# One product for values and router logits behind each norm, values kept in memory, the first sequence used in place, and down products with the last tile last

## The chip, the cores and the metric

The kernel runs on one core of a Trainium2 chip. The metric is device time in microseconds, as the median of several runs. TensorE (PE, with its weight loads as PEld), VectorE (DVE), ScalarE (ACT), GpSimd (POOL) and the DMA queue's engine SyncE (SP) each work through their own list of instructions in order and wait for each other through semaphores.

## What is computed

One transformer block over 16 sequences of 512 tokens of width 256, in float32: a layer norm, local attention with 16 heads of 16 (a token sees itself and the 128 tokens ahead of it), a mixture of 8 experts with 2 chosen for each token, a shared expert for all tokens, and the residual.

```python
xn = _layernorm(x)
# attention
q = (xn @ Wq.T + bq).reshape(B, S, 16, 16); k, v likewise
scores = where(local_mask, q k^T / 4, -10000.0)
attn = softmax(scores) + 1e-9
a = (attn v).reshape(B, S, 256) @ Wo.T + bo
# experts
logits = xn @ gate_w.T
_, idx = top_k(logits + beta, 2)
probs = sigmoid(logits at idx)
eo = (silu(xn gate_proj) * (xn up_proj)) down_proj     # for each expert
combined = sum over the two chosen of probs * eo
shared = (silu(xn sg) * (xn su)) sd
out = x + a + combined + shared
```

## The kernel before

The program is recorded by a Python function and put in order by a scheduler, which gives every instruction its place on its engine and every tile its buffer. A tile can only be taken when one of its pool's buffers has come free, and the scheduler may place other instructions first. Two pools are in PSUM: `bank_a` with five banks and `bank_b` with three, each bank 128 x 512 float32.

**Norm** (`norm`, L147 to L200). The sequences are normed in groups of three, sequence 0 alone ahead of all. For each sequence DVE takes statistics and writes `xn`, which is stored (`xn_d`, L181); TensorE turns it (L186), ACT copies it to `xT` (L187), which is stored to `xT_d` (L188). Then the router's logits: for each of four token tiles and two chunks of the width, a product of 8 columns (L194), and one DVE copy into `logits` (L198). `norm` is a generator; each `yield` ends a step.

**Attention** (`attention`, L645). For each sequence, `project` makes queries (L470), keys (L480) and values (L492, DVE adds the bias at L495) from a loaded `xT` (`load_turned`, L747). Queries go by DMA into the `spread` tiles (L454), values into the `halves` tiles (L462), where two runs of keys that share one tile stand side by side. A sequence has 20 steps: 4 groups of heads by 5 pieces of queries. A step is in four slots: scores (L531, DVE minimum and mask at L544, ACT exponential at L548), turning the probabilities (L556), the context's turn, and the values (L573, divided at L583 to L587). The next sequence's `project` parts run in steps 15 to 18 of the sequence ahead of it. At the end `output` multiplies by `wo` and adds into a sum tile `acc`.

**Shared expert** (`early`, L782). It loads `xT` and the sums so far (`load_sums`), runs `gate_up` (L720: for each of four tiles of the hidden width, gate and up products of 512 columns at L727, then `gated` on ACT and DVE at L715 to L717 into `h`), and then for each of four token tiles `add_product` (L737): four products of 256 columns into one `bank_b` tile, in the order of the hidden tiles (L740), and one DVE add (L745).

**Experts** (`experts`, L814): 135 blocks of 128 tokens. For each, weights are loaded (L825, 3 x 512 KB), tokens gathered (L835), turned (L845), and multiplied (L855, L873); results go to `y_d` (L880).

**Endings** (`endings`, L914): when all experts are done, each sequence's routed rows are gathered from `y_d` (L946) and added, weighted, into its sums (L923).

The order around these parts is that of one loop at the end of the function: in every slot of the attention it lets the norms and the router go on by up to one step (in 5 of 8 slots, until routing is done), the fill work (shared expert, then experts, then what is left of the shared expert) by 0.93 steps on average, and the endings by one:

```python
    for n, now[0] in enumerate(attention(range(B))):
        if not routed and n % 8 in (0, 2, 4, 6, 7):
            if next(behind, routed) is routed:
                routed.append(True)
        owed += pace
        while owed >= 1:
            owed -= 1
            next(fill, None)
        next(ends, None)
```

At the start x of sequence 0 is loaded, then the router's and the query weights, the key weights in eight transfers of 16-element runs (L224), value weights and the rest; sequence 0 is normed, its `xT` goes to memory and is loaded back for the attention and again for the shared expert. A second pass of the attention, for very low scores, stands behind a condition and is not run with these inputs.

Of the kernel before, what the change touches and what calls it, by code (L numbers as in the profile page):

```python
# [9 lines left out]
FP = mybir.dt.float32  # L10
I32 = mybir.dt.int32
AF = mybir.ActivationFunctionType
ALU = mybir.AluOpType
# [6 lines left out]
P = 128  # L20
# [23 lines left out]
def block_kernel(ctx: ExitStack, tc: tile.TileContext, a: dict, out: bass.AP):  # L44
# [22 lines left out]
    xT_d = dram.tile([B, P, KC, S], FP, tag="xT_d", name="xT_d")  # L67
    acc_d = dram.tile([TT * P, D], FP, tag="acc_d", name="acc_d")
# [24 lines left out]
    x_first = load_x([0])  # L93
    gw = load("gw", [P, KC, E], a["wv"][:, NH * DA :].rearrange("(c p) n -> p c n", p=P))
# [50 lines left out]

    logits = const.tile([P, TT, E], FP, tag="logits", name="logits")
    def norm(xs):  # L147
# [23 lines left out]
        for i, (b, x_sb) in enumerate(xs.items()):  # L171
# [10 lines left out]
            xT = two.tile([P, KC, S], FP, tag="hr", name="xT_new")  # L182
            for c in range(KC):
                tp = bank_a()
                for t in range(NT):
                    nc.tensor.transpose(tp[:, ts(t, P)], xn[:, t, ts(c, P)], ident)  # L186
                nc.scalar.copy(xT[:, c], tp)  # L187
            nc.sync.dma_start(out=xT_d[b], in_=xT)  # L188
            normed.add(b)
            yield  # L190
            pl = bank_b()
            for t in range(NT):
                for c in range(KC):
                    nc.tensor.matmul(  # L194
                        pl[:, ts(t, E)], lhsT=xT[:, c, ts(t, P)], rhs=gw[:, c],
                        start=c == 0, stop=c == KC - 1,
                    )
            nc.vector.tensor_copy(  # L198
                logits[:, ts(b, NT)], pl[:, : NT * E].rearrange("p (t e) -> p t e", t=NT)
            )  # L200

    normed = set()
    for _ in norm(x_first):
        pass
# [9 lines left out]


    wq = load("wq", [P, KC, D], a["wq"].rearrange("(c p) n -> p c n", p=P))


    wk = const.tile([P, KC, 2, P], FP, tag="wk", name="wk")
    for kc in range(KC):  # L220
        for j in range(4):
            c, s = j // 2, j % 2
            pick = lambda t: t.rearrange("p (r s d) -> p r s d", s=2, d=DK)[:, :, s]
            nc.sync.dma_start(out=pick(wk[:, kc, c]), in_=pick(a["wk"][ts(kc, P), j]))  # L224


    wv_by = part_tile(1, "wv_by")[:, : KC * NH * DA].rearrange("p (c n) -> p c n", c=KC)
    nc.sync.dma_start(
        out=wv_by, in_=a["wv"][:, : NH * DA].rearrange("(c p) n -> p c n", p=P)
    )  # L230
    bv_by = part_tile(2, "bv_by")[:, : NH * DA]
    nc.sync.dma_start(out=bv_by, in_=a["bv"].partition_broadcast(P))
    wv = const.tile([P, KC, 4, QA], FP, tag="wv", name="wv")
    bv = const.tile([P, 4, QA], FP, tag="bv", name="bv")

    def by_group(to, by):
        for i in range(4):
            heads = by.rearrange("p (c g s e) -> p c s g e", c=2, s=2, e=DA)[:, i // 2, i % 2]
            nc.gpsimd.tensor_copy(
                to[:, i, : QD * DK].rearrange("p (g d) -> p g d", d=DK), heads[:, :, :DK]  # L240
            )
            nc.gpsimd.tensor_copy(to[:, i, QD * DK :], heads[:, 0, DK:])

    for kc in range(KC):
        by_group(wv[:, kc], wv_by[:, kc])
    by_group(bv, bv_by)
    bq = load("bq", [P, 2], a["bq"])
    bk_by = load("bk_by", [P, 4], a["bk"])
    bk = const.tile([P, 2], FP, tag="bk", name="bk")
    nc.vector.tensor_tensor(bk, bk_by[:, 0::2], bk_by[:, 1::2], ALU.add)  # L250
    bo = load("bo", [P, D], a["bo"].partition_broadcast(P))
# [835 lines left out]
```

## Time and profile before

| | us |
|---|---|
| median of 3 runs (2170.99 to 2174.79) | 2172.68 |
| the profiled execution | 2172.1 |
| its span, first to last instruction | 2170.3 |
| mean granted TensorE clock | 0.984 |
| DMA moved | 390.10 MB, mean 180 GB/s |

Busy time of the costliest groups on TensorE, by line: expert gate and up (L855) 560.9 us, scores (L531) 326.3, context (L573) 205.5 and 193.0, expert down (L873) 273.9, shared gate and up (L727) 265.1, turning (L556) 188.2, shared down (L740, the group from `shared`) 137.6, values (L492) 62.0, logits (L194) 31.7.

A row of the profile names a source line, an engine, an operation and its tiles (out<-in), then how many there were, their busy time and mean length, and how long the engine had sat idle ahead of them, with what ended that wait. Every float32 product of the program shows as two records (two passes), so eight products of a sequence's values are sixteen records. The records of matmuls overlap; the distance from one group's start to the next one's is what a group takes.

### The profile page before, as it was taken

Reading aid. Unit: us, or ns where it says so; the run is one execution under the profiler, and the core shown is the slowest. Engines: PE = TensorE matmul, PEld = TensorE weight load, DVE = VectorE, ACT = ScalarE, POOL = GpSimd, SP = SyncE. Lnnn points to the kernel's source line nnn. Section 1 sums busy time; section 2 is a strip of 40 time slices with the busy share of each in tenths; the row PEclk is TensorE's granted clock in tenths of the full one; section 3 lists DMA queues with packets and bytes.
Section 4 is the critical chain, followed back from the end, with each engine's and each line's share of the span. In section 5 each row is a group of like instructions: output and inputs, shape, how many; then the busy total and the mean of one; then the engine's idle time right before and its main releaser. Section 6 shows DMA issues by size and latency. Waiting matters only on the chain.

```text
span 2170.3 us, 41414 instructions
## 1 busy us (share of the span) xinstructions
PE 2083.9 (96%) x13867; PEld 1815.9 (84%) x13867; DVE 1302.9 (60%) x5749; ACT 725.3 (33%) x1814; POOL 355.0 (16%) x451
## 2 busy tenths in 40 slices
PE   3999999999999999999999999999999999878988
PEld 2777877879999999989999898999999898555666
DVE  4776679965555555555555555555555555566665
ACT  1443322233333333333333333333334333122232
POOL 3101010011110111110111111111111111746220
PEclk8999999999999999999999999999999999999999
DMA  6534323136577666767676666666766664656530
GB/s 200 194 122 151 103 92 113 42 100 215 178 239 222 186 216 192 221 205 227 196 219 220 190 219 206 210 205 216 226 194 207 215 213 140 203 180 204 156 119 32
DMA packets 351278, 390.10 MB, mean 180 GB/s; under 512 B 94961, under 2 KB 266865, under 8 KB 351057
## 3 DMA queue, kind: packets, MB, share of 16 engines
q1 hardware_dynamic: 338432, 352.87, 51.8%
q0 software_dynamic: 12624, 34.49, 5.6%
q8 instruction: 114, 1.87, 0.4%
q14 instruction: 108, 0.88, 0.1%
HBM read 300.06 MB, written 59.64 MB: 166 GB/s over the span
## 4 chain that ended last, share of the span: by engine, by line
PE 86%; DVE 5%; DMA 3%; issue 3%; POOL 1%; SPq 1%; another core or an unknown queue 1%; ACT 0%; POOLq 0%; DVEq 0%; ACTq 0%
PE a L855 22%; PE a L531 11%; PE b L573 11%; PE b L873 10%; PE a L727 8%; PE b L740 6%; PE a L556 6%; PE a L480 2%; PE a L470 2%; PE b L492 2%; PE b L388 1%; PE b L845 1%; PE b L194 1%; DMA w<-in_gp 1%; POOL yg L946 1%
## 5 line engine op out<-in xcount | busy, mean ns | idle before, releaser
L548 ACT ACTIVATE probs<-probs,maxima 128x160 f32<-128x160 f32 (+4 forms) x1024 | 347.5, 401 | 679.3 <-DVE maxima L544 626.5
L855 PE MATMUL a<-xgT,w 128*128 128x128 f32 x4320 | 560.9, 276 | 1.9 <-DMA w<-in_gp 1.9
L855 PEld LDWEIGHTS a<-xgT,w 128*128 128x128 f32 x4320 | 524.7, 192 | 12.4 <-issue 7.5
L531 PE MATMUL a<-kT,spread 128*128 128x160 f32 (+4 forms) x2048 | 326.3, 297 | 4.5 <-DVE maxima L544 4.4
L531 PEld LDWEIGHTS a<-kT,spread 128*128 128x128 f32 x2048 | 291.1, 193 | 38.1 <-issue 21.1
L835 POOL DMA_INDIRECT xg<-xn_d,source x135 | 128.4, 951 | 1121.3 <-PE b L845 996.6
L544 DVE CUSTOM_DVE_ANT_0 probs<-a,window 128x160 f32<-128x160 f32 (+4 forms) x1024 | 255.1, 299 | 79.8 <-PE a L531 59.7
L727 PE MATMUL a<-xT,shared 128*128 128x512 f32 x512 | 265.1, 614 | 18.3 <-DMA xT<-xT_d 14.4
L587 DVE TENSOR_TENSOR cx<-b,rden 32x48 f32<-32x48 f32 (+1 forms) x1280 | 264.6, 207 | 22.3
L873 PE MATMUL b<-w,hr 128*128 128x256 f32 x1080 | 273.9, 381 | 0.0
L583 DVE TENSOR_SCALAR rden<-b 128x3 f32<-128x3 f32 (+1 forms) x320 | 50.9, 159 | 289.4 <-PE b L573 264.0
L573 PE MATMUL b<-halves,probsT 128*128 128x130 f32 x1152 | 205.5, 286 | 5.7 <-DVE cx L587 5.7
L873 PEld LDWEIGHTS b<-w,hr 128*128 128x128 f32 x1080 | 187.9, 190 | 17.2 <-issue 1.4
L573 PEld LDWEIGHTS b<-v,probsT 128*128 128x128 f32 x1280 | 185.5, 192 | 14.1 <-issue 11.3
L556 PE MATMUL a<-ident,probs 128*128 128x128 f32 x1216 | 188.2, 274 | 7.2 <-ACT probsT L561 3.5
L573 PE MATMUL b<-v,probsT 128*128 128x65 f32 x1280 | 193.0, 257 | 0.0
L573 PEld LDWEIGHTS b<-halves,probsT 128*128 128x128 f32 x1152 | 169.6, 193 | 26.9 <-issue 22.5
L556 PEld LDWEIGHTS a<-ident,probs 128*128 128x128 f32 x1216 | 149.7, 142 | 49.8 <-issue 25.5
L716 DVE SCALAR_TENSOR_TENSOR hr<-hr,a 128x512 f32<-128x512 f32 x135 | 92.7, 687 | 122.5 <-ACT hr L715 121.8
L740 PE MATMUL b<-shared,h 128*128 128x256 f32 x512 | 137.6, 396 | 19.0 <-DVE h L717 12.8
L946 POOL DMA_INDIRECT yg<-y_d,slots x128 | 122.9, 960 | 171.6 <-DVE acc L923 72.0
L561 ACT COPY probsT<-a 128x512 f32<-128x512 f32 x192 | 110.4, 575 | 86.2 <-PE a L556 71.8
(134 smaller groups left out, 2058.4 us busy)
## 6 DMA issues: line engine op xcount, KB each, us to landing
w<-in_gp SPq DMA_DIRECT2D x135, 512.0 KB
w<-in_up SPq DMA_DIRECT2D x135, 512.0 KB
w<-in_dp SPq DMA_DIRECT2D x135, 512.0 KB
y_d<-y SPq DMA_DIRECT2D x135, 128.0 KB
xT<-xT_d SPq DMA_DIRECT2D x32, 512.0 KB
acc_d<-acc SPq DMA_DIRECT2D x32, 512.0 KB
acc<-acc_d SPq DMA_DIRECT2D x32, 512.0 KB
halves<-v SPq DMA_DIRECT2D x96, 97.5 KB
```

Of the source, the lines that this page charges most:

```text
L531: nc.tensor.matmul(ps[:, at : at + e - f], lhsT=spreads[s][:, u].rearrange("p g q -> p (g q)"), rhs=w["kT"][:, c, f:e], start=True, stop=True,
L544: nc.vector.tensor_tensor_reduce(out=pr[:, span], in0=ps[:, span], in1=window[:, WIN - (e - f) :], scale=-SCALE, scalar=-MASKED, op0=ALU.a ...
L548: nc.scalar.activation(pr[:, span], pr[:, span], AF.Exp, bias=least, scale=-1.0)
L556: nc.tensor.transpose(tp[:, ts(i, P)], pr[:, ts(i, P)], ident)
L573: nc.tensor.matmul(av[:, n * QA : (n + (2 if split else 1)) * QA], lhsT=pT[:, ts(i, P)], rhs=rhs, start=i == 0, stop=i == count - 1 - coun ...
L587: nc.vector.tensor_tensor(to[rows, :, s], tot[rows, :, ts(g, DK)], rden[rows, :n].unsqueeze(2).to_broadcast([Q, n, DK]), ALU.mult,)
L727: nc.tensor.matmul(ps, lhsT=wt[:, c, ts(m, P)], rhs=xT[:, c], start=c == 0, stop=c == KC - 1,)
L740: nc.tensor.matmul(po[:, :D], lhsT=l, rhs=r, start=n == 0, stop=n == len(parts) - 1)
L835: nc.gpsimd.indirect_dma_start(out=g, out_offset=None, in_=xn_d, in_offset=bass.IndirectOffsetOnAxis(ap=source[:, i : i + 1], axis=0),)
L855: nc.tensor.matmul(hidden[i][which][:, ts(m, P)], lhsT=weights[i, which][:, c, ts(m, P)], rhs=turned[i][:, c], start=c == 0, stop=c == KC - 1,
L873: nc.tensor.matmul(po[:, :D], lhsT=made[i][:, ts(m, P)], rhs=weights[i, 2][:, m], start=m == 0, stop=m == MC - 1,)
L946: nc.gpsimd.indirect_dma_start(out=y[:, 2 * i + k], out_offset=None, in_=y_d, in_offset=bass.IndirectOffsetOnAxis(ap=slots[:, n, k : k + 1 ...
```

## The change

- **Values with logits.** `wv` gets 268 columns: 4 x 65 for the values and 8 for the router. `norm` now multiplies each token tile of `xT` by it (two products of 268 columns for a tile in `bank_b`); DVE adds the bias into a value tile and ACT copies the 8 logits. The values are stored to memory (`v_d`), and the attention loads them (`load_values`) where it made them before. Except for sequence 0, the value tile of a norm is taken from the four `acc` buffers. `norm` has two more `yield`s for each sequence.
- **First sequence.** Its x comes in four transfers; all weights are asked for ahead of everything else; key weights come in one transfer and are summed on GpSimd. Its queries, keys and values are made in its norm from the `xT` tile, and the shared expert takes the same tile; nothing of it is loaded back.
- **Order in the attention.** For sequence 0 the `halve` transfers are issued one piece at a time with its first five scores, not all ahead of them; for the others they stay in the last steps of the sequence ahead. `spread` of group 1 goes ahead of the scores of its step.
- **Down products.** `add_down` takes two token tiles at a time, each with its own `bank_b` tile: three products for the one, three for the other, then the fourth of both.

```diff
+    v_d = dram.tile([B, P, NT, 4, QA], FP, tag="v_d", name="v_d")
...
-    x_first = load_x([0])
-    gw = load("gw", [P, KC, E], a["wv"][:, NH * DA :].rearrange("(c p) n -> p c n", p=P))
+    x_first = part_tile(0, "x_in").rearrange("p (t d) -> p t d", d=D)
+    for t in range(NT):
+        nc.sync.dma_start(out=x_first[:, t], in_=a["x"][0, ts(t, P)])
...
+    wv = const.tile([P, KC, 4 * QA + E], FP, tag="wv", name="wv")
...
+    nc.gpsimd.tensor_tensor(wk, wk_by[:, :, :, 0], wk_by[:, :, :, 1], ALU.add)
...
             nc.sync.dma_start(out=by_tile(xn_d, b), in_=xn)
-            xT = two.tile([P, KC, S], FP, tag="hr", name="xT_new")
+            tag = "xT" if first else "hr"
+            xT = two.tile([P, KC, S], FP, tag=tag, name="xT_new")
...
+            if first:
+                first(xT)
             nc.sync.dma_start(out=xT_d[b], in_=xT)
-            normed.add(b)
             yield
-            pl = bank_b()
+            if first:
+                v = two.tile([P, NT, 4, QA], FP, tag="v", name="v")
+            else:
+                v = four.tile([P, NT * 4 * QA], FP, tag="acc", name="v_new").rearrange(
+                    "p (t i n) -> p t i n", t=NT, i=4
+                )
             for t in range(NT):
+                pv = bank_b()
                 for c in range(KC):
                     nc.tensor.matmul(
-                        pl[:, ts(t, E)], lhsT=xT[:, c, ts(t, P)], rhs=gw[:, c],
+                        pv[:, : 4 * QA + E], lhsT=xT[:, c, ts(t, P)], rhs=wv[:, c],
                         start=c == 0, stop=c == KC - 1,
                     )
...
+                nc.vector.tensor_tensor(
+                    v[:, t], pv[:, : 4 * QA].rearrange("p (i n) -> p i n", i=4), bv, ALU.add
+                )
+                nc.scalar.copy(logits[:, b * NT + t], pv[:, 4 * QA : 4 * QA + E])
+                if t % 2:
+                    yield
+            nc.sync.dma_start(out=v_d[b], in_=v)
+            normed.add(b)
...
+    def load_values(w):
+        w["v"] = two.tile([P, NT, 4, QA], FP, tag="v", name="v")
+        nc.sync.dma_start(out=w["v"], in_=v_d[w["b"]])
...
+                if b == bs[0] and group == 0:
+                    halve(w, r)
...
+                    elif n == 2:
+                        load_values(behind)
+                        lane_sums(behind)
...
+    def add_down(acc, h):
+
+        for t0 in range(0, NT, 2):
+            order = [(t, m) for m0 in (0, MC - 1) for t in (t0, t0 + 1)
+                     for m in range(m0, max(MC - 1, m0 + 1))]
+            po = {t0: bank_b(), t0 + 1: bank_b()}
+            for n, (t, m) in enumerate(order):
+                nc.tensor.matmul(
+                    po[t][:, :D], lhsT=h[m][:, ts(t, P)], rhs=wd[:, m],
+                    start=m == 0, stop=m == MC - 1,
+                )
+                if m == MC - 1:
+                    nc.vector.tensor_tensor(acc[:, t], po[t][:, :D], acc[:, t], ALU.add)
+                if n % 2:
+                    yield
...
-        xT, acc = load_turned(b), load_sums(b)
+        xT, acc = first_xT.pop(b, None) or load_turned(b), load_sums(b)
...
+    def first_projections(xT):
+        project_queries(ws[0], xT)
+        spread(ws[0], 0)
+        project_keys(ws[0], xT)
+
+    for _ in norm({0: x_first}, first_projections):
+        pass
```

## The prediction

> **What bounds the kernel now.** I read the granted clock first (one core, 0.984 over the span), then the busy time by engine, then the share of each engine in stretches of time, then TensorE's timeline wherever a stretch was thin.
>
> ```profile
> PE 2083.9 (96%) x13867; PEld 1815.9 (84%) x13867; DVE 1302.9 (60%) x5749; ACT 725.3 (33%) x1814; POOL 355.0 (16%) x451
> ...
> 0.00:54.00 54.00, 20.60 (x66) 13.59 (x67) 23.57 (x98) 7.83 (x13) 19.71 (x67) 0.88 0.68 200
> ...
> 100.00:150.00 50.00, 50.00 (x293) 38.78 (x293) 39.59 (x176) 19.60 (x45) 2.36 (x1) 1.00 0.48 157
> ...
> 900.00:1200.00 300.00, 300.00 (x2244) 281.40 (x2243) 167.16 (x764) 110.99 (x286) 41.48 (x47) 1.00 0.69 215
> ...
> 1848.00:2085.00 237.00, 197.09 (x885) 140.74 (x885) 150.77 (x603) 54.92 (x140) 121.70 (x132) 0.90 0.59 184
> 2085.00:2171.00 86.00, 77.19 (x396) 57.40 (x395) 52.37 (x228) 22.86 (x56) 1.95 (x3) 0.98 0.17 52
> ```
>
> The columns after the stretch are its length, then busy us and instruction counts of PE, PEld, DVE, ACT and POOL, then granted clock, DMA share and GB/s. PE is full from 100 to 1848 us and thin in two places, the first 54 us and the last 320. A busy PE need not be a fast one, so I also added its records up at their spacing in a row: 8 records of 512 columns take 3.43 us (0.43 each), 8 of 260 take 1.75 (0.22), 16 of 128 take 1.79 (0.11). That gives 198 of 200 us between 100 and 300, 592 of 600 between 600 and 1200, but 15 of 54 at the start, 172 of 237 between 1848 and 2085, and 75 of 86 behind that. So in the middle TensorE's stream is the time: a product taken out there is worth its spacing. At the two ends waits set the time.
>
> The start, on TensorE and on the DMA queue:
>
> ```profile
> 24.88 5.08 PE L470 MATMUL a<-xT,wq 128*128 128x512 f32 x8 [9.23 <-DMA xT<-xT_d]
> 29.79 3.60 PE L480 MATMUL a<-xT,wk 128*128 128x512 f32 x8
> 33.23 3.67 PE L492 MATMUL b<-wv,xT 128*128 128x260 f32 x16
> 36.73 1.20 PE L531 MATMUL a<-kT,spread 128*128 128x32 f32 x8
> 52.31 5.49 PE L727 MATMUL a<-xT,shared 128*128 128x512 f32 x6 [14.37 <-DMA xT<-xT_d]
> ```
> ```profile
> 12.46 0.32 SPq L188 DMA_DIRECT2D xT_d<-xT_new  x1
> ...
> 35.30 11.40 SPq L462 DMA_DIRECT2D halves<-v  x18
> ...
> 47.38 0.54 SPq L749 DMA_DIRECT2D xT<-xT_d  x1
> ```
>
> The first sequence's turned tokens are in SBUF at 12.4 us, go to memory, and are waited for twice: 9.2 us before the queries, and 14.4 us before the shared expert, because its load (47.38) stands behind eighteen halves transfers that hold the queue for 11.4 us.
>
> **The change part by part.** The sum is made against the profiled execution: span 2170.3 us, 2172.1 with what lies around it; the median of the runs is 2172.7, so 0.6 apart.
>
> *Logits inside the value product.* Eight products of 8 columns per sequence go (16 records), and eight of 260 columns become 268.
>
> ```profile
> 80.47 1.85 PE L194 MATMUL b<-gw,xT_new 128*128 128x8 f32 x16
> 82.17 1.11 PE L740 MATMUL b<-shared,h 128*128 128x256 f32 x4
> ...
> L194 PE MATMUL b<-gw,xT_new 128*128 128x8 f32 x256 | 31.7, 258 | 0.1
> ```
>
> From 80.47 to the next group at 82.17 is 1.70 us for 16 records, 0.106 each: as much as a 128-column product, so the weight load sets it. Here a rule disagrees: the Trainium skill, "TensorE: Matmul & The Clock Gate", section "Back-to-back issue gap", lists about 60 cycles (a 25 ns floor) for up to 64 columns. By it the 16 records would cost 0.4 us a sequence, and the edit would bring 15 x (0.4 - 0.1) = 4.5 us. The row is of this very product, so it decides: 15 sequences (the first is counted with the start) x 1.70 = 25.5 out, 15 x 16 records x 8 columns x 0.84 ns = 1.6 back in. **-24 us**, all in stretches that are full.
>
> The value products themselves (3.5 us a sequence) only move, from the attention loop into the norms. ACT gets 64 copies of 8 columns; its nearest row, 128x2 out of the same kind of bank (L521), takes 171 ns, so 11 us on an engine 33% busy. DVE loses 16 logit copies (190 ns).
>
> *The first sequence in place.* The new order on SP is: x in four pieces, all weights, then norm results. PE's order: 8 transposes, queries, keys, values, scores, then shared products, with no load between. Transposes begin at about 9 (9.7 before; the statistics now start on the first piece), xT is there at about 11.5, queries take 5.1 (half clock at first, as in the row above), keys 3.4, values 3.6, scores 0.9: shared products begin at **24.6** instead of 52.3, 27.7 us earlier. What must be ready: wk now needs one GpSimd add over 512 columns (the 260-column add takes 0.76-0.83, so 1.6) behind the sorting of wv; its 1.6 MB are in by 10 at the 140 to 296 GB/s of the first 25 us, so wk is ready near 14, keys start near 16.6. The spread transfers now stand behind the shared weights: 3.6 MB in all, landed by 20; scores are due at 23.7.
>
> What is late next: x of sequences 1 to 3. Before, they were loaded from 16.8, and 14 us of DVE work on them (14.0 busy between 25 and 40) hid in the wait. Now they stand behind v_d and six halves transfers (values at 24.2, then 0.6 each), issued from 28.6 and in from 31. The statistics and normalising then share DVE with scores and gating: some 17 us of DVE work stand ahead of the first new xn in DVE's order, which puts it near 49; PE, dense from 24.6, wants its transposes at 44.5. So 5 lost there, about 2 when sequence 1's xT comes back from memory (its load stands behind acc_d's store), and 2 for DVE waiting at x; before lost 2.1 between 54 and 100. **-27.7 + 9 - 2.1 = -20.8 us**, between -28 (no stall) and -8.
>
> *PSUM banks in the norm stage.* There are three b banks. The new down products hold two at once across steps; a value tile holds one until DVE has added (427 ns) and then ACT has copied. The skill speaks against the change here: "PSUM — Partial Sum Buffer", section "PSUM bank collisions raise a hardware error", says no two engines may touch one bank's same quadrant together, readers included; so the two reads go one behind the other, and ACT's instruction indeed waits for DVE. By the old row (L492's two tiles ran in 1.75 us without a gap, PE waited for L495 once, 0.5 us) the price is 0. By the rule the bank is held 0.43 + 0.17 plus two hand-overs and both engines' queues, which I put at 2.2 us; in PE's new order twenty takings of a bank follow a value tile by less than that, and the shortfalls add up to 12. I take **+8**, ends 0 and 20 (other engine work, DVE 79% busy between 100 and 150, may be in front).
>
> *Values through memory.* 16 stores and 15 loads of 532 KB, two xT loads less: some 15.5 MB on 390. At 211 GB/s a load is 2.5 us. The DMA engines are 68% busy in that stretch, and PE waited for expert weights 1.9 us in all, so the cover is the slack of double-buffered weights. **+1**; 38 (15 x 2.5) if none of it were covered. The load is asked for one step ahead of the halves transfers that read its tile; should it be late by its 2.5 us, these hold SP that long, but in SP's and PE's orders more than 25 us of stream lie between them and the products that read the halves. v_new shares the four acc buffers: nothing, unless a shared sum must wait.
>
> *Down products.* The fourth h tile is now read behind six products instead of three: 3 x 0.43 = 1.3 us more for gating. PE waited for that tile 12.8 us in four waits (longest 7.1), all behind 1848. **-3**, ends 0 and -10.
>
> *The tail.* A norm now has five steps per sequence where it had three, so routing comes later, two more sequences get their shared expert before the experts, and the last expert product moves from attention sequence 14.0 to 14.5 in PE's order. The routed adds move from 13.9-15.45 to 14.6-16.0. The stretch with those adds lost 65 us of stream (237 - 172), the dense one behind it 11. The adds are the same 128 and now reach to the end: I carry the same 76 us over, **0**, ends -8 and +25.
>
> Sum: -24 - 20.8 + 8 + 1 - 3 = -38.8; 2172.1 - 38.8 = **2133 us**.
>
> **Rivals.** (1) *Only the stream counts*: the start's gain is given back because DVE, short of the work it did in the wait, holds PE through the first norm group. For it: DVE 79% busy in 100-150. Against: PE was 99% streamed there with that DVE load. Start -8, banks +12: -24 - 8 + 12 + 1 - 3 = -22, 2150 us. (2) *Everything overlaps*: no bank stalls, start -28, down -5, tail -5: -62, 2110 us. (3) *Slower: the routed adds spill over the end.* One sequence's adds need eight gathers at 1.25 us (0.95 and 0.30 before the next) on POOL, 10 us, and two yg buffers. There are some 150 steps left where 128 are needed. From the fourth sequence that is still open when attention ends, 40 us stand uncovered and the gain is gone; six would give about 2155 + 20 = 2175. Against it: the new order has the last add ahead of the last output product. (4) *Nothing*: had logits been hidden and the start been bound by transfers that remain, within 0.2% of 2172; the full stream speaks against it.
>
> **How the numbers follow.** Forecast 2133 (2120 to 2145): 0.62; rival 1: 0.17; rival 2: 0.15; rival 3: 0.04; rival 4: 0.02. 0.2% (4.3 us) is about what a measurement can tell from no change. Faster 0.94, same 0.02, slower 0.04. The range takes in rivals 1 and 2 up to their own centres and a little beyond: 2108 to 2156.
>
> **What would show it.** Right: no product of 8 columns; shared products from about 25 us; PE records between 150 and 350 still at 97% or more of their spacing; a last yg add in the last 15 us. Wrong: a PE gap over 8 us before 60; PE waiting for ACT's logit copy for more than 20 us in all; PE waiting for v or w in every sequence; PE under 60% in the last 200 us.

## The result and the profile after

The kernel before took 2172.36 us (median of 4 runs, 2170.99 to 2174.79), the changed kernel 2134.53 us (4 runs, 2131.55 to 2140.34): a ratio of 0.9828, with a 95% interval of 0.9805 to 0.9851. The prediction was 2133 us. The profiled execution of the changed kernel took 2131.55 us, its span is 2129.8 us, 40.5 less than before; the medians are 37.8 apart.

The same two views as before, first the busy time by engine on the page, then the shares of the engines in stretches of time (stretch, length, busy us and counts of PE, PEld, DVE, ACT and POOL, granted clock, DMA share, GB/s):

```profile
PE 2061.2 (97%) x13611; PEld 1786.7 (84%) x13611; DVE 1294.1 (61%) x5732; ACT 734.2 (34%) x1880; POOL 353.3 (17%) x438
```
```profile
0.00:54.00 54.00, 43.58 (x180) 28.82 (x181) 32.79 (x140) 20.57 (x44) 21.72 (x55) 0.97 0.68 214
100.00:150.00 50.00, 50.00 (x244) 36.13 (x243) 35.73 (x152) 19.75 (x48) 2.23 (x6) 1.00 0.38 126
900.00:1200.00 300.00, 299.32 (x2244) 279.56 (x2244) 164.38 (x760) 113.05 (x291) 39.70 (x52) 1.00 0.69 218
1880.00:2130.00 250.00, 204.23 (x900) 143.63 (x899) 156.07 (x624) 54.33 (x136) 122.33 (x126) 0.90 0.56 171
```

The first 54 us hold 43.6 us of PE where they held 20.6. The norm stage is still full, with fewer records (244 for 293), and no record of 8 columns is left. The expert stage has not moved. The last stretch is as thin as it was: 82% busy at a clock of 0.90, against 83% and 0.90.

The start on TensorE's timeline (start, length, then the group; in brackets the idle time ahead of it and what ended it):

```profile
7.67 2.21 PE L242 MATMUL a<-ident,xn 128*128 128x128 f32 x8 [7.67 <-DVE xn L230]
9.70 4.56 PE L489 MATMUL a<-xT_new,wq 128*128 128x512 f32 x8
14.09 3.60 PE L499 MATMUL a<-xT_new,wk 128*128 128x512 f32 x8
17.53 3.78 PE L257 MATMUL b<-wv,xT_new 128*128 128x268 f32 x16
21.14 1.20 PE L543 MATMUL a<-kT,spread 128*128 128x32 f32 x8
22.18 2.74 PE L730 MATMUL a<-xT_new,shared 128*128 128x512 f32 x6
...
44.74 1.66 PE L242 MATMUL a<-ident,xn 128*128 128x128 f32 x8 [2.26 <-DVE xn L230]
```

Both waits for an `xT` from memory (9.2 and 14.4 us) are gone, and the shared products begin at 22.2 us where they began at 52.3. What is late next is the `xn` of the next norm group: 2.3 us at 44.7.

To see where the 40.5 us came from, I added up TensorE's records at their spacing again (0.83 ns a column, at least 0.11 us a record), by stretch, each record in the stretch in which it begins. The rest of a stretch is lost: waiting, half clock, or a record missing from the trace. (The prediction and the expectations count a record on the edge of two windows in both, which makes their lost figures up to 3 us smaller: their 54 us up to 1880 are 56.5 here.) The last stretch begins at 1848 us before and at 1880 after, soon after the last expert.

| us lost | 0-100 | 100-300 | 300-600 | 600 to last stretch | last stretch | sum | stream |
|---|---|---|---|---|---|---|---|
| before | 41.7 | 1.8 | 9.5 | 17.1 | 75.6 | 145.7 | 2024.6 |
| after | 18.3 | 2.1 | 18.0 | 18.1 | 75.1 | 131.7 | 1998.1 |
| difference | -23.4 | +0.3 | +8.5 | +1.0 | -0.5 | -14.0 | -26.5 |

### The profile page after: what moved, and what is told of

Its sections match the earlier page's. It is cut to its first block, busy times and chain, and to the rows that moved or that the text cites. A ratio compares the mean times of both kernels' runs of the same rounds, so it can differ in the third digit from the quotient of the medians.

```text
span 2129.8 us, 40970 instructions
## 1 busy us (share of the span) xinstructions
PE 2061.2 (97%) x13611; PEld 1786.7 (84%) x13611; DVE 1294.1 (61%) x5732; ACT 734.2 (34%) x1880; POOL 353.3 (17%) x438
## 5 line engine op out<-in xcount | busy, mean ns | idle before, releaser
L543 PEld LDWEIGHTS a<-kT,spread 128*128 128x128 f32 x2048 | 291.5, 193 | 41.6 <-issue 23.4
L599 DVE TENSOR_TENSOR cx<-b,rden 32x48 f32<-32x48 f32 (+1 forms) x1280 | 264.5, 207 | 22.2
L730 PE MATMUL a<-xT,shared 128*128 128x512 f32 x480 | 245.4, 605 | 6.2 <-issue 1.8
L595 DVE TENSOR_SCALAR rden<-b 128x3 f32<-128x3 f32 (+1 forms) x320 | 50.9, 159 | 288.0 <-PE b L585 264.3
L585 PEld LDWEIGHTS b<-v,probsT 128*128 128x128 f32 x1280 | 186.1, 193 | 17.5 <-issue 13.2
L585 PEld LDWEIGHTS b<-halves,probsT 128*128 128x128 f32 x1152 | 169.3, 193 | 30.5 <-issue 24.3
L568 PEld LDWEIGHTS a<-ident,probs 128*128 128x128 f32 x1216 | 149.5, 142 | 46.9 <-issue 30.4
L718 ACT ACTIVATE hr<-a 128x512 f32<-128x512 f32 x135 | 79.9, 592 | 144.6 <-PE a L873 144.6
```

Of the source, the lines that this page charges most:

```text
L543: nc.tensor.matmul(ps[:, at : at + e - f], lhsT=spreads[s][:, u].rearrange("p g q -> p (g q)"), rhs=w["kT"][:, c, f:e], start=True, stop=True,
L568: nc.tensor.transpose(tp[:, ts(i, P)], pr[:, ts(i, P)], ident)
L585: nc.tensor.matmul(av[:, n * QA : (n + (2 if split else 1)) * QA], lhsT=pT[:, ts(i, P)], rhs=rhs, start=i == 0, stop=i == count - 1 - coun ...
L599: nc.vector.tensor_tensor(to[rows, :, s], tot[rows, :, ts(g, DK)], rden[rows, :n].unsqueeze(2).to_broadcast([Q, n, DK]), ALU.mult,)
L730: nc.tensor.matmul(ps, lhsT=wt[:, c, ts(m, P)], rhs=xT[:, c], start=c == 0, stop=c == KC - 1,)
```

## The experiments

Twelve runs were made, in four series; the runs of one series share their runs of the kernel before. In the first series that kernel took 2141.1 us, in the others 2168.8 to 2172.6. The record does not tell what was different in the first series (it numbers the chips 0, 10, 5 and again 0), so times are compared within a series where that is possible. Every version changes the changed kernel in the one place shown.

| run | series | kernel before | this, median (range) | ratio, 95% interval |
|---|---|---|---|---|
| e1 logits apart | 1 | 2141.1 | 2115.2 (2114.3-2117.8) | 0.9882 (0.9860-0.9904) |
| e2 queries from memory | 1 | 2141.1 | 2101.4 (2099.7-2103.2) | 0.9822 (0.9800-0.9844) |
| e3 shared expert from memory | 1 | 2141.1 | 2105.5 (2103.8-2106.2) | 0.9835 (0.9813-0.9858) |
| e4 old down order | 1 | 2141.1 | 2091.3 (2087.6-2093.2) | 0.9767 (0.9742-0.9791) |
| e5 values twice | 2 | 2171.6 | 2144.3 (2141.1-2146.3) | 0.9877 (0.9856-0.9898) |
| e6 banks held longer | 2 | 2171.6 | 2130.2 (2126.3-2132.6) | 0.9808 (0.9785-0.9832) |
| e7 norm in three steps | 2 | 2171.6 | 2129.5 (2128.6-2133.1) | 0.9805 (0.9785-0.9824) |
| e8 six gather tiles | 2 | 2171.6 | 2145.2 (2144.5-2146.9) | 0.9881 (0.9861-0.9901) |
| e10 changed kernel again | 3 | 2168.8 | 2137.7 (2135.2-2140.9) | 0.9854 (0.9834-0.9873) |
| e11 old down order again | 3 | 2168.8 | 2133.1 (2128.9-2135.8) | 0.9825 (0.9806-0.9845) |
| e9 gathers spread | 3 | 2168.8 | 2136.1 (2134.4-2139.2) | 0.9849 (0.9830-0.9867) |
| e12 half the gathers | 4 | 2172.6 | 2076.0 (2075.0-2079.1) | 0.9557 (0.9537-0.9576) |

Their lost time, worked out in the same way from each trace (the last stretch begins at 1880 us; for e7 at 1800, near its last expert):

| us lost | 0-100 | 100-300 | 300-600 | 600 to last stretch | last stretch |
|---|---|---|---|---|---|
| e1 | 19.1 | 1.9 | 11.9 | 20.1 | 38.4 |
| e2 | 26.5 | 2.1 | 16.8 | 17.7 | 36.5 |
| e3 | 30.5 | 2.7 | 17.3 | 18.8 | 37.0 |
| e4 | 19.5 | 1.9 | 16.2 | 18.2 | 37.3 |
| e5 | 25.9 | 2.7 | 16.7 | 19.0 | 76.9 |
| e6 | 19.6 | 2.5 | 17.6 | 17.5 | 72.5 |
| e7 | 19.0 | 6.3 | 14.2 | 20.3 | 73.4 |
| e8 | 19.9 | 2.5 | 16.7 | 19.2 | 86.4 |
| e10 | 18.6 | 2.2 | 17.4 | 18.0 | 81.6 |
| e11 | 19.0 | 2.2 | 16.3 | 18.7 | 79.8 |
| e9 | 18.8 | 2.6 | 17.8 | 17.9 | 78.3 |
| e12 | 23.0 | 2.3 | 16.9 | 17.9 | 16.0 |

The stream is 2024.6 us in e1, as before the change, and 1998.1 in all others.

**e1, the logits apart again.**

```diff
+            pl = bank_b()
+            for t in range(NT):
+                for c in range(KC):
+                    nc.tensor.matmul(
+                        pl[:, ts(t, E)], lhsT=xT[:, c, ts(t, P)], rhs=wv[:, c, 4 * QA :],
...
-                        pv[:, : 4 * QA + E], lhsT=xT[:, c, ts(t, P)], rhs=wv[:, c],
+                        pv[:, : 4 * QA], lhsT=xT[:, c, ts(t, P)], rhs=wv[:, c, : 4 * QA],
...
-                nc.scalar.copy(logits[:, b * NT + t], pv[:, 4 * QA : 4 * QA + E])
```

> One part undone: the logits again as eight products of 8 columns per sequence with one DVE copy, the value product at 260 columns; everything else as changed. My theory (the 8-column product costs a weight load, 0.106 us a record, in a full stream): 16 sequences x (1.70 - 0.11) = +25 us, so 2157 to 2161 us against 2134.5 of the changed kernel, with the loss in the stretches where the norms run (up to about 500 us) and none behind them. Rival (the short product is worth its 25 ns, or hides): +3 to +5, so 2138 to 2140.

The changed kernel was not in this series; e4 stands in for it, since it has the same stream (1998.1 us) and, stretch by stretch, within 2 us the same losses up to 1880. Beside e4, e1 is 23.8 us slower; if e4 is itself 4.5 us faster than the changed kernel, as in series 3, 19 us are left. Either way the rival with 3 to 5 us falls. Both are net figures: e1 also loses 4.3 us less than e4 between 300 and 600. The group among e1's groups of instructions (out<-in, shape, count, busy us, mean ns of one, idle ahead):

```profile
L257 PE MATMUL b<-wv,xT_new 128*128 128x8 f32 x256 | 29.8, 251 | 0.2 <-ACT xT_new L243 0.2
```

With the 1.7 us that the 8 columns cost in the merged product, the 256 records are worth (23.8 + 1.7) / 256 = 0.100 us each, or 0.082 from the 19: less than half of the mean length that the row gives. A product is worth the distance between records, not their length. The table above takes 0.11 us for these records and so does not measure it again, but it fits: at 0.025 the full stretch from 100 to 300 us of e1, with 128 of them, would come out 11 us short, and it comes out full (198.1 of 200). TensorE's timeline of e1 shows the distance itself, 1.70 us for 16 records or 0.106 each:

```profile
125.24 1.85 PE L257 MATMUL b<-wv,xT_new 128*128 128x8 f32 x16
126.94 2.00 PE L267 MATMUL b<-wv,xT_new 128*128 128x260 f32 x8
```

**e2, the first sequence's projections from memory.**

```diff
+            nc.sync.dma_start(out=xT_d[b], in_=xT)
             if first:
+                xT = load_turned(b)
                 first(xT)
-            nc.sync.dma_start(out=xT_d[b], in_=xT)
```

> One part undone: the first sequence's queries, keys and values are made from an xT that was stored and loaded back; the shared expert takes that loaded tile too. My theory: TensorE waits for a store and a load of 0.5 MB behind the transposes, some 6 us at the queues' rates of the start (before it was 9.2 with other transfers ahead), all of it before the shared products, so these begin at 28 instead of 22.2 and the time is 2140 to 2142. Rival (the wait hides, since DVE with the next norm group sets when TensorE can go on): shared products later, but the time within 2 us of 2134.5 and the wait for xn at 44.7 gone.

10.1 us slower than e4, and the lost time differs most within the first 100 us (26.5 against 19.5; 18.3 in the changed kernel), so 7 to 10 us are the load's. The theory had the size and not the way. TensorE's timeline and that of the DMA queue, of e2:

```profile
22.48 6.55 PE L489 MATMUL a<-xT,wq 128*128 128x512 f32 x8 [12.53 <-DMA xT<-xT_d]
...
37.90 2.74 PE L730 MATMUL a<-xT,shared 128*128 128x512 f32 x6
```
```profile
10.77 1.06 SPq L243 DMA_DIRECT2D xT_d<-xT_new  x1
12.09 2.09 SPq L85 DMA_DIRECT2D x_in<-in_x  x2
18.56 0.34 SPq L766 DMA_DIRECT2D xT<-xT_d  x1
18.95 2.11 SPq L85 DMA_DIRECT2D x_in<-in_x  x4
```

The wait is 12.5 us and not 6, since the load is issued 7.8 us after its store; for 3.6 of these SyncE waited until the store had landed. The shared products begin 15.7 us later than in the changed kernel, but only 7 to 10 of that reach the end: in this order x of the next sequences is loaded from 12.1 us on (26.0 in the changed kernel), so TensorE has no wait for `xn` at 45 us and streams 71.4 of the 75 us from 25 to 100, against 66.4. About half of the delay was paid for by what the changed kernel is short of.

**e3, the shared expert from memory.**

```diff
-        xT, acc = first_xT.pop(b, None) or load_turned(b), load_sums(b)
+        xT, acc = load_turned(b), load_sums(b)
```

> One part undone: the shared expert loads the first sequence's xT back instead of taking the tile in place; queries, keys and values still in place. Before, this load stood behind eighteen halves transfers and cost a wait of 14.4 us. My theory: what cost the time was the place of the load in the queue, not the load; now only six halves transfers are ahead of it, each 0.6 us, so it comes at about 29 and TensorE loses 5 to 8 us between scores and shared products: 2140 to 2143. Rival A (the load itself is what costs, wherever it stands): +14, 2149. Rival B (hidden by attention work that TensorE can do): 2134 to 2136.

14.1 us slower than e4, rival A's number; in the first 100 us e3 loses 11 us more than e4 and 12 more than the changed kernel. That lies above my theory and under the rival or on it. From e3's TensorE timeline and DMA queue:

```profile
22.21 1.20 PE L543 MATMUL a<-kT,spread 128*128 128x32 f32 x8
40.07 4.93 PE L730 MATMUL a<-xT,shared 128*128 128x512 f32 x6 [16.66 <-DMA xT<-xT_d]
```
```profile
23.30 3.77 SPq L479 DMA_DIRECT2D halves<-v  x6
27.13 4.30 SPq L85 DMA_DIRECT2D x_in<-in_x  x6
31.47 1.27 SPq L766 DMA_DIRECT2D xT<-xT_d  x1
```

The load is asked for behind the halves and six loads of x, at 31.5 us, and TensorE goes on 8.6 us later; I had counted only the halves ahead of it. When it was asked for, 8.1 of the 16.7 us of waiting were over: its place in the queue was a good part of the cost here too, with other transfers in front. TensorE then finds nothing else to do from 23.4 to 40.1.

**e4 and e11, the old order of the down products.**

```diff
-        yield from add_down(acc, h)
+        for t in range(NT):
+            po = bank_b()
+            for m in range(MC):
+                nc.tensor.matmul(
+                    po[:, :D], lhsT=h[m][:, ts(t, P)], rhs=wd[:, m],
+                    start=m == 0, stop=m == MC - 1,
+                )
+                if m == MC // 2 - 1:
+                    yield
+            nc.vector.tensor_tensor(acc[:, t], po[:, :D], acc[:, t], ALU.add)
+            yield
```

> One part undone: shared down products in the old order, one bank and one token tile at a time, the last hidden tile read by the fourth product. My theory (from the prediction): the old waits for h behind 1848 us, 12.8 us in four, come back in part, +3 us (0 to +10), so 2137; PE's wait for h of gating returns to some 10 us. Rival: those four waits came from what DVE did in the endings and not from the order, so the time stays at 2134.5 within 2 us.

> The old order of the down products once more, beside the changed kernel on one chip. Its first run lost the same stream up to 1880 us as the changed kernel (53 against 54), so my theory now: the order of the down products is worth nothing, the two within 4 us of each other. Rival 1 (the prediction): the old order 3 us slower, up to 10. Rival 2 (the first run's ratio, 0.977 against 0.983): the old order 12 us faster.

In series 3 the old order takes 2133.1 us and the changed kernel 2137.7: 4.5 us less, with ranges that overlap by 0.6 us. So the new order brings nothing, and may cost a little; the 12 us of the ratios in the first run came from comparing across series. The wait for `h` that the expectation looked for did not follow the order either: behind 1880 us TensorE waited 7.2 us for it in e4 and 4.7 in e11, and 5.5 in e10, which has the new order.

**e5, the values stored and loaded twice.**

```diff
+            nc.sync.dma_start(out=v_d[b], in_=v)
             nc.sync.dma_start(out=v_d[b], in_=v)
...
         nc.sync.dma_start(out=w["v"], in_=v_d[w["b"]])
+        nc.sync.dma_start(out=w["v"], in_=v_d[w["b"]])
```

> One cost doubled: each sequence's values are stored to memory twice and loaded twice, the second load on top of the first. My theory (double-buffered weights cover it): +2 us at most, 2134 to 2137, with PE waiting for v or for expert weights no more than 3 us in all. Rival (transfers of this size push expert weights late): 15 loads x 2.5 us = +38, or with a part of it covered at least +10, and waits for w in every sequence.

2144.3 us: more than my theory allowed, 9.8 above the changed kernel's first run and 14 above e6 in its own series. By its number that is near the rival's lower end, but not by its way: from 100 to 1880 us e5 loses 38.4 us, the changed kernel 38.2, and PE waits for expert weights 0.3 us there in all, so fifteen more loads and stores cost nothing in that stretch. Before 100 us it loses 7.6 us more than the changed kernel. The first sequence's second store stands ahead of the loads of x and moves them from 26.04 to 27.89 us; the wait for `xn` grows from 2.3 to 4.4 us and that for sequence 1's `xT` from 1.7 to 3.8. Those two make 4.3; behind the second the granted clock is 0.50 for 6.8 us (from 75.3), which costs 3.4 more. Such a half clock comes without this edit too: e12 has it for 6.8 us from 47.8 and 3.4 from 75.1, and loses 23.0 there. The rest, some 2 us beside the changed kernel and 4 beside e6, lies in the last stretch, which differs by more than that from run to run.

**e6, the banks held longer.**

```diff
-                nc.scalar.copy(logits[:, b * NT + t], pv[:, 4 * QA : 4 * QA + E])
+                for _ in range(4):
+                    nc.scalar.copy(logits[:, b * NT + t], pv[:, 4 * QA : 4 * QA + E])
```

> The disputed cost raised: ACT copies each tile's 8 logits four times over instead of once, so that each value tile holds its PSUM bank some 0.5 us longer, in 64 tiles. The prediction put +8 us on banks; the trace of the changed kernel shows 198 of 200 us streamed between 100 and 300, so my theory is now that banks have slack: 2134 to 2137. Rival (banks are just in balance, and the prediction's reckoning of twenty takings per stretch was right in kind): 64 x 0.5 x a third to a half = +10 to +20, with PE waiting for ACT's copy in the profile.

2130.2 us, and 2.5 us lost between 100 and 300 instead of 2.1; PE waited for ACT's copies once, 1.0 us. A bank is now held 1.34 us behind its last product, in the middle of the 64 tiles, where it was 0.67 in the changed kernel. That is covered, and the rival falls.

**e7, a norm in three steps a sequence.**

```diff
-                if t % 2:
-                    yield
```

> One part undone: a norm has three steps a sequence again instead of five, so that routing is done earlier and experts end about half a sequence of attention earlier. My theory: the lost time of the tail goes with the number of routed adds, not with where they begin, so the last stretch loses the same 75 us within 5, and the time is 2131 to 2138; what TensorE lost ahead of routing (about 17 us between 300 and 600, against 8.5 before the change) moves with the routing. Rival: the later experts cost the tail, and putting them back gives 10 to 20 us, 2115 to 2125. Other rival: denser norm work costs the banks, +8 or more.

2129.5 us, a little under what my theory held for likely and beside e6 no different. The last stretch, now from 1800, loses 73.4 us: the same loss (72.5 in e6) though the experts end some 70 us earlier, so where they end is not what costs. The banks do feel the denser norms: 6.3 us lost between 100 and 300. PE's waits of e7 between 60 and 300 (what waited for what, us in total, times, longest):

```profile
PE b L257 <- ACT logits L264: 2.4, 2, 2.0
PE a L728 <- DMA xT<-xT_d: 1.7, 1, 1.7
PE b L583 <- ACT logits L264: 0.4, 1, 0.4
```

VectorE's add comes 2 to 3 us late for three tiles near 120 us, and these hold their banks 3.6 to 4.4 us behind the last product. So a stall of the kind that the prediction put at 8 us exists, at 3 to 4 us, where holds get that long; with the two extra steps they did not.

**e10, the changed kernel again, as a measure.**

> The changed kernel once more, as the measure for the runs beside it: on one chip (before at 2141) four kernels lost only 36 to 38 us of stream behind 1880 us, on another (before at 2172) the changed kernel and three others 72 to 77, with the same instructions. My theory: chip and not change sets this, so the stream lost up to 1880 is 54 us within 2 on any chip, and the time is 2132 to 2138 where before is near 2172, or 2089 to 2094 where before is near 2141. Rival: the change has a loss of its own behind 1880 that the four others escaped, and then it stays at 75 on a chip on which before is near 2141.

56.2 us lost up to 1880 and 81.6 behind, 6 us more in the tail than in the first profile. The kernel before was near 2170 here, where theory and rival expect the same, so this run does not part them. e11 does for the old down order: one program lost 37.3 us behind 1880 in series 1 and 79.8 in series 3. For the changed kernel itself it is not shown.

**e8 and e9, two attempts at the tail.**

```diff
-                y = two.tile([P, 4, D], FP, tag="xn", name="yg")
+                turns[0] += 1
+                y = part_tile(turns[0] % 3, "yg").rearrange("p (t d) -> p t d", d=D)
```

> An attempt at the tail: the tiles into which routed rows are gathered come from the six buffers of the part tiles instead of two, so that GpSimd's gathers (it waits 39 us for DVE's adds in the changed kernel) can run ahead of DVE. If the pair of buffers couples GpSimd and DVE: 10 to 20 us less, 2115 to 2125, with PE streaming 190 or more of the last 250 us. My theory is less hopeful: DVE works in order and its adds stand where the program put them, so fewer waits of GpSimd but 2128 to 2136. Rival: the part tiles are held by others then, and it is slower.

```diff
+                        yield
+                        if (i, k) == (1, 0) and added:
+                            add()
-                yield
-                yield
-                if added:
-                    add()
                 added.append((b, half, acc, y))
-                yield
-                yield
```

> An attempt at the tail: the routed gathers are asked for one in a step instead of four at once, and added four steps later; same gathers, same adds. In the traces of the changed kernel VectorE stood still for about 7 us three times behind 1880, each time until a train of gathers was through (at 1893.6, 1933.9, 2017.9). If trains of gathers cause these stalls: 15 to 30 us less where the tail lost 75, and little where it lost 37. If each gather costs its time wherever it stands: within 4 us of the changed kernel. Rival: the later gathers make the adds wait, 5 to 10 us slower.

Neither helped. With six tiles the time is 2145.2 us, 15 above e6 and e7 and so on the rival's side; GpSimd still waits 42.8 us for adds, and the last stretch loses 86.4. The other edit gives 2136.1 beside 2137.7: nothing. But it did not spread the gathers: in e9's trace they still follow each other at 0.3 us in trains of 4 to 16, as in the changed kernel, so e9 says nothing about trains. What the stalls look like is best seen where one program ran in two series. VectorE's timeline at the same place of the program, in e11 (series 3):

```profile
1884.36 0.68 DVE L719 SCALAR_TENSOR_TENSOR h<-h,a 128x512 f32<-128x512 f32 x1
1892.82 0.16 DVE L595 TENSOR_SCALAR rden<-b 128x3 f32<-128x3 f32 x1 [7.79 <-remote]
1892.90 0.48 DVE L951 SCALAR_TENSOR_TENSOR acc<-yg,prob,acc 128x256 f32<-128x256 f32 x1
```

and in e4 (series 1), the same kernel:

```profile
1884.01 0.68 DVE L719 SCALAR_TENSOR_TENSOR h<-h,a 128x512 f32<-128x512 f32 x1
1884.61 0.15 DVE L595 TENSOR_SCALAR rden<-b 128x3 f32<-128x3 f32 x1
1884.68 0.48 DVE L951 SCALAR_TENSOR_TENSOR acc<-yg,prob,acc 128x256 f32<-128x256 f32 x1
```

The instructions ahead of this place run alike, 0.35 us apart. Then VectorE stands still for 7.8 us in one series and not at all in the other. The profile names no engine of the core as what ended it ("remote").

It is not a gather that comes late. The L951 row is the sixth add of the endings, so by count it reads the sixth gather, and the trace of e11 shows that gather's packets on their way from 1883.7 to 1884.5 us and signals of its landing at 1884.5. The row that waited (L595) reads a product of TensorE, and TensorE's timeline of e11 shows it done in time:

```profile
1883.73 0.33 PE L585 MATMUL b<-v,probsT 128*128 128x65 f32 x2
...
1889.32 1.08 PE L730 MATMUL a<-xT,shared 128*128 128x512 f32 x2
1894.10 1.86 PE L543 MATMUL a<-kT,spread 128*128 128x128 f32 x6 [3.71 <-DVE h L720]
```

The trace also keeps when each semaphore was raised. TensorE's for this product was raised at 1892.80 us, 8.7 us behind the product's end, and six more of its products, all done by 1890.4, were signalled between then and 1893.2; the last of a train of twelve gathers had moved its rows until 1892.0. In e4 the same product ends at 1883.7 and is signalled at 1883.7. So VectorE waited for a late signal of finished work. Waits that end in "remote" add up, over all engines, to 22.8 us in the kernel before, 13.2 in the changed kernel, 46.9 in e10, 40.1 in e11, and 31 to 60 in e5 to e9. In each of these they lie between the first and the last of the routed gathers; e1 to e4 have none. What holds the signals back is not shown. The last run asks whether the gathers have to do with it.

**e12, half of the gathers.**

```diff
-                        acc[:, t], y[:, 2 * i + k], prob[:, k, n : n + 1], acc[:, t],
+                        acc[:, t], y[:, 2 * i], prob[:, k, n : n + 1], acc[:, t],
...
-                    for k in range(2):
+                    for k in range(1):
                         nc.gpsimd.indirect_dma_start(
```

> Half of the routed gathers are left out: only the row of the first chosen expert is gathered, and it is added twice, so the result is another; the 128 adds and everything else stay. It tells what the tail is bound by. If the adds on VectorE and their place in its order set it (the prediction's picture, the same adds and so the same loss): the stream lost behind 1880 us stays within 8 us of what the changed kernel loses on such a chip (about 75 where before is near 2170, about 37 where it is near 2141). If the gathers set it, by their 1.25 us on GpSimd or by when they land: 25 to 40 us less where the loss was 75, so 2095 to 2112; 10 to 20 less where it was 37.

2076.0 us. Shares of the engines in the last stretch, of e12:

```profile
1880.00:2074.00 194.00, 183.29 (x916) 133.17 (x914) 158.48 (x631) 56.77 (x142) 63.65 (x65) 0.99 0.58 178
```

and of the changed kernel in series 3:

```profile
1880.00:2136.00 256.00, 205.99 (x898) 145.75 (x896) 155.71 (x621) 54.29 (x136) 121.93 (x126) 0.88 0.55 166
```

VectorE does the same work (158 and 156 us), GpSimd half (64 and 122), and the stretch is 62 us shorter: 16.0 us lost where 81.6 were, more than the 25 to 40 that were foreseen for this case. So the adds are not what binds the tail; the gathers, or what comes with them, are. The 62 us are not the price of 64 gathers. e12's trace has no wait that ends in "remote", where e10 has 46.9 us. Beside e4, which has all the gathers and no such wait either, e12 loses 21 us less (16.0 and 37.3, in two series): a third of a microsecond for a gather. Its trains are of 2 to 4 gathers; those of e4 are of 10 to 40. Whether the number of gathers or their trains hold the signals back, and why not in series 1, stays open, and the run does not part GpSimd's time from the landings.

No version of the whole computation beat the changed kernel by much: the old down order is 4.5 us below it in one series.

## Why the prediction was right, step by step

| step | predicted us | measured us | from |
|---|---|---|---|
| logits in the value product | -24 | -24.8 | stream -26.5, without the first sequence's 1.7 (by 0.11 us a record again, so not a measurement of its own); 19 to 24 by e1 |
| first sequence in place | -20.8 | -25.1 | lost -23.4, with that 1.7 |
| PSUM banks | +8 | +0.3 | lost, 100 to 300 |
| values through memory, down order | +1, -3 | +1.0 | lost, 600 to the last stretch |
| routing | not in the sum | +8.5 | lost, 300 to 600 |
| tail | 0 | -0.5 | lost, last stretch |
| sum | -38.8 | -40.5 | spans |

**Logits.** Right, and for its reason. The row of the product itself (0.106 us a record) against the rule of 25 ns decided between 24 and 4.5 us; undoing the merge gave 0.08 to 0.10 us a record. The page was in fact not against it: the section that the prediction cites (the Trainium skill, "TensorE: Matmul & The Clock Gate", "Back-to-back issue gap") gives its table for a product alone and says that at small widths it counts too little, because the weight load is not in it.

**The first sequence.** Right in kind, and small by 4.3 us. Shared products begin at 22.2 us (24.6 predicted), because queries take 4.4 us instead of 5.1 and transposes begin at 7.7 instead of 9. What was to be late next came: a wait for `xn` at 44.7 (2.3 us against 5), sequence 1's `xT` (1.7 against 2), VectorE at x (2.2 against 2); the stretch from 25 to 100 lost 8.6 us of the 9 foreseen, though half clock behind the first wait (granted clock 0.50 from 45.6 to 49.0 us) is part of these and was not in the sum. e2, e3 and e5 show both halves: what stands between asking for a load and having it was the cost, and x of the next sequences is the limit now. Undone one at a time, the two loads cost 7 to 10 and 11 to 14 us; both at once was not tried.

**Banks.** The term that was mis-sized: +8, measured 0. I had put a hold at 2.2 us. TensorE, VectorE and ScalarE at two tiles of the changed kernel:

```profile
126.73 1.97 PE L257 MATMUL b<-wv,xT_new 128*128 128x268 f32 x8
127.83 0.43 DVE L261 TENSOR_TENSOR v_new<-b,bv 128x260 f32<-128x260 f32 x1 [0.15 <-PE b L257]
128.30 0.17 ACT L264 COPY logits<-b 128x8 f32<-128x8 f32 x1 [1.16 <-DVE v_new L261]
```

The first tile's four records end at 127.80, the add follows at once and the copy within 0.05 us of the add, so the bank is free 0.67 us behind its last product (and 1.73 behind the start of its first). In half of the 64 tiles it is the same, in the longest 2.1 us. The two reads do go one behind the other, as the rule weighed there says, and they cost next to nothing: e6 doubled this hold and lost 0.4 us more there. The whole group of the changed kernel, with its wait:

```profile
L257 PE MATMUL b<-wv,xT_new 128*128 128x268 f32 x256 | 64.0, 392 | 0.5 <-ACT logits L264 0.4
```

**Routing.** Not foreseen: +8.5 us between 300 and 600. VectorE is the full engine there before and after (24.4 of 25 us), but in the changed kernel TensorE has nothing left for 3 us when the router needs it, where no wait of the kernel before is longer than 0.7 us in that stretch (3.0 in all):

```profile
391.04 2.07 PE L334 MATMUL a<-r_c,out_prev 128*128 128x512 f32 x2 [2.96 <-DVE r_c L332]
```

That is TensorE's timeline of the changed kernel; behind it four records of 512 columns take 3.6 us where they take 1.7 at full clock. With the two shorter gaps ahead of it (1.1 and 0.6 us) and the slow records up to 398, this is about 4.7 us of waiting and 3 of half clock, out of the 18.0. e1 has half the wait there and loses 11.9 us in the stretch; with the old down order it is 16.2 and 16.3. Why the router finds less to hide behind in the changed order was not settled: e7, which routes earlier, still loses 14.2. That this term fills the place of the +8 for banks is luck.

**Values through memory** cost nothing where the weights stream (e5). **Down order**: the waits for the fourth h tile were 3.4 us in all in the first profile against 12.8, but not because of the order (5.5 in e10, 4.7 with the old order in e11), and the time did not follow them. The step that failed is "-3"; it counted waits in a stretch that something else set.

**The tail** kept its loss, 75.1 for 75.6, so 0 was right, but the picture behind it was not: the prediction named the adds, and e12 shows that it is not they. Where no signals come late, one program loses 37 us there instead of 80, so about half of what was carried over went with the late signals, which no sum contained. Both profiles have such waits (22.8 and 13.2 us); that the two losses come out alike is in part luck. Rival 3 had the right resource, GpSimd with its gathers, and the wrong consequence: the endings keep up with the attention at the price of its pace, and do not spill over. (Its last figure does not follow: six open sequences at 10 us each on 2133 would be 2193.)

## What to carry to other kernels

Where TensorE's records stand at their spacing, price a product by the distance between such records in this trace, and look for short products that still pay a weight load; where they do not, ask what the stretch waits for before counting any wait in it, since removing another one gives nothing (the down order). A load from memory of something that is already on chip costs its store and what stands ahead of it in its queue as well, so taking it away is worth all that, less what then becomes late. Where a stretch is thin and no engine is full, leaving out half of the suspected work (the gathers) told in one run what two rearrangements did not. Check in the trace that an edit of the order did change the order (e9 did not), and set the end of the awaited work beside the end of the wait: they can be 8.7 us apart.

## What the runs showed of the hardware

**One program, two times.** The old down order took 2091.3 us in series 1 and 2133.1 in series 3, the kernel before 2141.1 and 2168.8. Up to 1880 us the two traces of the one program lose 55.8 and 56.2 us; behind it 37.3 and 79.8, in the stretch with the gathers. A ratio to the kernel before does not take this out (0.9767 and 0.9825 for the one kernel), so versions with such gathers are to be compared within a series. What the traces show of the difference is that signals of finished work come late in the one (by 8.7 us at the place above, with waits of 40.1 us of this kind in all) and not in the other; its cause is open.

**The clock falls on short waits.** A wait of 2.96 us, with gaps of 1.1 and 0.6 us in the 6 us before it, was followed by 512-column records of 0.9 us; the stretch of the changed kernel:

```profile
375.00:400.00 25.00, 20.33 (x90) 14.65 (x89) 22.48 (x75) 5.62 (x14) 0.00 (x0) 0.86 0.16 46
```

The granted clock is 0.86 there. The same wait, 1.51 us long in e1, was followed by records at 0.43 us and a clock of 1.00. The length of one wait does not decide: behind e1's of 1.79 us at 47.0 the clock was 0.50 for 6.8 us, behind e7's of 2.08 us at 1760.3 it stayed at 1.00. The Trainium skill, "TensorE: Matmul & The Clock Gate", section "Part 1: The HAM clock gate", puts the fall at an idle window of about 3.4 us; here less idle time in one piece was enough.
